# A four-layer graph network: layer 2's attention weights formed transposed, and the norms' deviations by logarithm and exponential

## The chip, the cores and the metric

The kernel runs on one core of a Trainium2 chip. The metric is the time of one execution on the device in microseconds (us), the median of several runs. One core has five engines that run beside each other, each with its own queue that is worked through in order: TensorE (PE, matrix products; its weight loads, PEld, overlap the products), VectorE (DVE), ScalarE (ACT), GpSimd (POOL) and SyncE (SP, which only issues transfers here). TensorE writes into eight banks of PSUM; the other data lie in SBUF.

## The reference

A batch of 32 graphs has 512 nodes with 128 features each, and all graphs share one 512x512 adjacency matrix. Four layers follow one another, each of the form `x = x + layer(relu(layernorm(x)))`. What the change touches is layer 2 and the layer norms:

```python
def _layernorm(x, axis=-1, eps=1e-5):
    m = jnp.mean(x, axis=axis, keepdims=True)
    v = jnp.var(x, axis=axis, keepdims=True)
    return (x - m) / jnp.sqrt(v + eps)

def _L2_gnn_ref(h, adj, W, a, bias):
    Wh = jnp.einsum('bnf,fo->bno', h, W)
    f1 = Wh @ a1;  f2 = Wh @ a2
    e = leaky_relu(f1[:, :, None] + f2[:, None, :], negative_slope=0.2)
    e = jnp.where(adj[None] > 0, e, -9e15)
    attention = softmax(e, axis=2)
    return elu(jnp.einsum('bij,bjo->bio', attention, Wh) + bias)
```

Layer 0 pairs nodes in another way and takes the softmax over the other axis. Layer 1 is the same kind of attention as layer 2, with the weights multiplied by the adjacency matrix, then a norm, a product with the adjacency matrix, a two-layer perceptron with a norm of its own, and a residual. Layer 3 applies one 512x512 matrix, the same for all graphs, to a projection.

## The kernel before

One graph is one item of work: its 512 nodes are four blocks of 128 (C = 4, H = 2), so that a tile is 128 partitions x 4 x 128 values, and such a tile fills one PSUM bank. Each item goes through `layer0`, `layer1`, `layer2`, `layer3`; all of x stays in SBUF (`xs`, one slot for each of the 32 items).

**The order of the work** isn't the order of the loops. Each step of a layer is handed to a planner (`Plan.op`) with its engine, a length in us, what it reads and what it writes. `Plan.run` then places all steps, those that can begin first, among equals the one with the earliest due time (`turn`), and the engines' queues are written in that order. The layers of different items are chains with begin times (`GAPS`); layer 1 follows layer 0 six items later, layer 2 twelve and layer 3 sixteen items later (`LAGS`). At most 20 chains are open at a time (`WINDOW`). `port=` marks steps of DVE and POOL that the planner does not let overlap. Where the planner sees PE idle for over 0.6 us, it puts throw-away products there (`idle_products`, L334).

**The norm** in front of each layer (`preln`): DVE takes mean and variance with four bn_stats and four bn_aggr (L511, L513); POOL adds the epsilon (L523) and raises to the power -0.5 (L525, `inv_dev`); the normalised tile `xn` comes from POOL (four instructions, L560), or from ACT for the first eight items of layer 0 (L545); four PE transposes (`turn_op`, L421) and an ACT Relu out of PSUM (L570) give `hT`. The perceptron's norm in layer 1 also uses `inv_dev`, and layer 1's own norm raises to -0.5 by POOL at L892.

**Attention** of layers 1 and 2 (`attend`): `project_scored` (L595) gives `h` with two more columns, the scores f1 and f2. Four PE transposes of the column f2, each broadcast over 128 columns, lay f2 out along the free axis in each partition (`repeated`, tile `prow`). Then, for each block of rows ib:

- DVE adds mask and f2 and takes the row's maximum in one instruction (L622, tile `y`),
- ACT forms the leaky ReLU (L647, f1 as bias), then the exponential with the row's maximum as bias and the row's sum accumulated (L655),
- PE turns the 128x512 block by four transposes into a bank (L421, tile `pt`), since a product needs the weights with columns j on the partitions,
- the bank is copied to `pT`: in layer 1 by DVE, times the adjacency matrix (L664); in layer 2 by ACT (L412, blocks 0 and 1) or DVE (L414, blocks 2 and 3),
- PE adds four products into `po` (L675).

`layer2` then multiplies `po` by the reciprocal of the sums (L952, L955), adds the bias on POOL (L956) and forms the elu on ACT, DVE and POOL (L960 to L962). The helper lines L421, L412, L414 and L675 are shared by layers.

An fp32 product counts as two records of MATMUL in the trace, a transpose as one: L675 has 2048 records for 2 layers x 32 items x 16 products.

Of the kernel before, what the change touches and what calls it, by code (L numbers as in the profile page):

```python
# [37 lines left out]
P = 128  # L38
# [8 lines left out]
AHEAD = 6  # L47

# [209 lines left out]
def kernel(  # L258
# [36 lines left out]
    assert F == P and C == 4 and NE % P == 0 and B >= AHEAD  # L295
# [3 lines left out]
    sm = ctx.enter_context(tc.tile_pool(name="sm", bufs=8))  # L299

# [7 lines left out]
    def small(name, shape=(P, C)):  # L308
        return sm.tile(list(shape), F32, name=name, tag=name)

# [12 lines left out]
    scored = room("scored", 6, (P, C, P2))  # L323
# [31 lines left out]
    nc.vector.memset(minus1, -1.0)  # L355
    one_b = const("one_b", (P, 1), BF16)
# [3 lines left out]
    xs = const("xs", (P, B, C, P))  # L360
# [20 lines left out]
    none = const("none", (P, C))  # L381
    maxbT = const("maxbT", (P, C))
# [14 lines left out]
    v_x = [Value() for _ in range(B)]  # L397
# [4 lines left out]
    v_offT, v_adiag, v_adiag_rep = Value(), Value(), Value()  # L402
# [4 lines left out]
    def load_x(b):  # L407
        load(lambda: xs[:, b], x[b].rearrange("(c p) f -> p c f", p=P), [v_x[b]], 1.0)
# [94 lines left out]
    def variances(src, reads):  # L503

        mv = Value()

        def emit():
            st = small("st", (P, C, 6))
            mv.own = small("mv", (P, C, 2))
            for c in range(C):  # L510
                nc.vector.bn_stats(st[:, c, :], src(c))  # L511
            for c in range(C):
                nc.vector.bn_aggr(mv.own[:, c, :], st[:, c, :])  # L513

        dve(1.1, emit, reads, [mv])
        return mv

    def inv_dev(mv):
        rstd = Value()

        def emit():
            ve = small("ve")
            nc.gpsimd.tensor_scalar(ve, mv.own[:, :, 1], LN_EPS, 1.0, ALU.add, ALU.mult)  # L523
            rstd.own = small("rstd")
# [5 lines left out]
    def preln(b, engine):  # L530

        src = xs[:, b]
        mv = variances(lambda c: src[:, c, :], [v_x[b]])
        rstd = inv_dev(mv)
        shift = Value()
        xn = value(by_act if engine is ACT else by_pool, "xn")
        if engine is ACT:

            def emit_shift():
                shift.own = small("shift")  # L540
                nc.vector.scalar_tensor_tensor(shift.own, mv.own[:, :, 0], -1.0, rstd.own, ALU.mult, ALU.mult)
# [10 lines left out]
        else:  # L552

            def emit_shift():
                shift.own = small("shift")
# [30 lines left out]
    def project_scored(hT, w_ext, reads):  # L586

        h = parts(scored, "h", 2)
        for k in range(2):
            pt = value(banks, "proj")  # L590

            def emit(k=k, pt=pt):
# [6 lines left out]
                ACT, 0.26, lambda k=k: h[k].t[:, 2 * k : 2 * k + 2, :],  # L599
# [10 lines left out]
    def attend(h, src, v_src, v_h, weights, v_weights):  # L610


        prow = repeated(lambda k: h[0].t[:, k, P + 1 : P2], h)
        y = [value(scores, "y") for _ in range(C)]
        rmax = Value()
        top = [Value() for _ in range(C)]
        for ib in range(C):

            def emit(ib=ib):
                if ib == 0:  # L620
                    rmax.own = small("rmax")
                nc.vector.tensor_tensor_reduce(  # L622
                    wide(y[ib].t), wide(prow.t), bias[:, ib, :], 1.0, LOWEST, ALU.add, ALU.max,
# [3 lines left out]
            op(DVE, 0.61, emit, [prow, v_bias], [y[ib], top[ib]])  # L627
# [12 lines left out]
        dve(0.08, emit_nmax, [ntop], [nmax], port=1)  # L640
        ssum = [Value() for _ in range(C)]
        po = parts(banks, "po", C)
        for ib in range(C):
# [18 lines left out]
            if weights is not None:  # L662
                pT = value(turned, "pT")
                op(DVE, 0.6, lambda ib=ib, pt=pt, pT=pT: nc.vector.tensor_mul(pT.t, pt.t, weights[:, :, blk(ib)]),  # L664
                   [pt, *v_weights], [pT])
            elif ib < H:
                pT = value(by_act, "pT")
                copy_op(ACT, 0.49, lambda pT=pT: pT.t, lambda pt=pt: pt.t, [pt], [pT])
            else:
                pT = value(turned, "pT")  # L670
                copy_op(DVE, 0.6, lambda pT=pT: pT.t, lambda pt=pt: pt.t, [pt], [pT])
# [15 lines left out]
    def layer0(b):  # L687
# [165 lines left out]
        dve(0.33, lambda: nc.vector.tensor_add(xs[:, b, 0:H, :], xs[:, b, 0:H, :], first[0].t[:, 0:H, :]),  # L853
            first, [v_x[b]])
        dve(0.33, lambda: nc.vector.tensor_add(xs[:, b, H:, :], xs[:, b, H:, :], terms()[:, :, 0, :]),
            second, [v_x[b]])
        op(POOL, 0.7, lambda: nc.gpsimd.tensor_add(xs[:, b, H:, :], xs[:, b, H:, :], rest.t[:, 0:H, :]),
# [3 lines left out]
    def layer1(b):  # L861
# [26 lines left out]
        rr = Value()  # L888

        def emit_rr():  # L890
            rr.own = small("rstd")
            nc.gpsimd.tensor_tensor(rr.own, ve.own, mhalf, ALU.pow)  # L892

        op(POOL, 1.0, emit_rr, [ve], [rr])
# [43 lines left out]
        op(DVE, 0.6, lambda: nc.vector.scalar_tensor_tensor(xs[:, b], res.t, 0.0, xs[:, b], ALU.max, ALU.add),  # L938
# [3 lines left out]
    def layer2(b):  # L942
        hT, _ = preln(b, POOL)
        h = project_scored(hT, w2_ext, [v_w2])
        po, ssum = attend(h, lambda: h[0].t[:, :, P], h, h, None, None)
        v1 = value(by_dve, "v1")

        rs = Value()

        def emit_rs():  # L950
            rs.own = small("rs")
            nc.vector.reciprocal(rs.own, ssum[0].own)  # L952

        dve(0.1, emit_rs, ssum, [rs])
        dve(0.6, lambda: nc.vector.tensor_mul(v1.t, po[0].t, per_chunk(rs.own)), [*po, rs], [v1])  # L955
# [6 lines left out]
        op(POOL, 1.25, lambda: nc.gpsimd.tensor_add(xs[:, b], xs[:, b], em.t), [em], [v_x[b]], port=1)  # L962


    def layer3(b):
# [6 lines left out]
        op(POOL, 1.25, lambda: nc.gpsimd.tensor_add(xb.t, xs[:, b], row_of(B_L3)), [v_x[b], v_rows], [xb], port=1)  # L972
# [22 lines left out]
    def prepare():  # L995
# [24 lines left out]
        for ib in range(C):  # L1020
            dve(0.31, lambda ib=ib: nc.vector.tensor_scalar(
                bias[:, ib, :], bias[:, ib, :], 0.0, NEG, ALU.is_le, ALU.mult), [], [v_adj[ib], v_bias], port=1)
        score_weights(lambda: wt_p.t[:, 0, :], wt_p, a1[:, 0:2], v_a1, w1_ext[:, P:P2], v_w1)
# [338 lines left out]
```

## Time and profile before

| | |
|---|---|
| time, median of 3 runs | 1062.31 us (1062.3 to 1063.7) |
| span of the profiled execution | 1062.1 us |
| PE busy | 1041.7 us, 98% |
| DVE busy | 868.5 us, 82% |
| ACT busy | 780.5 us, 73% |
| POOL busy | 776.2 us, 73% |
| granted TensorE clock, mean | 0.996 |
| first output of layer 2 (`v`, L955) | 214 us after the start |
| first output of layer 3 (`yo`, L991) | 311 us |
| last inputs of layer 0 used (`hs`, L805) | 778 us |
| last output of layer 2 / layer 3 | 1040 / 1058 us |

The profile is of one execution; its own time is taken as its span, which is 0.2 us under the median of the runs. A "group" is all instructions of one source line with the same operands: busy time of the group, mean duration of one, and the engine's idle time just before them with what ended it. Where instructions of an engine overlap, the busy time is less than the count times the mean. The "chain" is the work that ended last, followed back from the end.

### The profile page before, as it was taken

The numbers are of one execution on the slowest core, as the hardware profiler recorded it, in microseconds if no ns is written. First come the engines' busy times: TensorE is split into PE (matmuls) and PEld (weight loads), VectorE is DVE, ScalarE is ACT, GpSimd is POOL, SyncE is SP. The second block draws the span as 40 slices with busy tenths as digits, with TensorE's granted clock in tenths as the row PEclk, the third lists the DMA queues.
The fourth block names the chain that finished last, engine by engine and source line by source line (L and its number), as shares of the span: only waits on it lengthen the run. The fifth ranks groups of instructions, "written<-read, shape, count | busy, mean of one in ns | idle before, by whom it ended". The sixth has DMA issues, their size and how long they took to land.

```text
span 1062.1 us, 25166 instructions
## 1 busy us (share of the span) xinstructions
PE 1041.7 (98%) x8475; PEld 966.0 (91%) x8475; DVE 868.5 (82%) x3694; ACT 780.5 (73%) x2024; POOL 776.2 (73%) x1140
## 2 busy tenths in 40 slices
PE   7899999999999999999999999999999999999998
PEld 7789789989999999999999999999899999999997
DVE  7799999989988878888888888888888877766752
ACT  6768897789877777777877777787777777767751
POOL 4489577778787777787778778777877666576772
PEclk9899999999999999999999999999999999999999
DMA  6400000000010000000000000000000000000001
GB/s 181 96 12 2 1 2 21 2 12 11 2 31 2 21 21 21 22 21 12 2 12 11 12 12 12 11 2 11 12 11 11 11 11 11 11 22 11 22 24 37
DMA packets 56912, 20.49 MB, mean 19 GB/s; under 512 B 21584, under 2 KB 56272, under 8 KB 56784
## 3 DMA queue, kind: packets, MB, share of 16 engines
q1 hardware_dynamic: 56784, 18.90, 7.2%
q8 instruction: 67, 1.10, 0.5%
q14 instruction: 61, 0.50, 0.2%
HBM read 10.43 MB, written 8.39 MB: 18 GB/s over the span
## 4 chain that ended last, share of the span: by engine, by line
PE 88%; DVE 4%; POOL 3%; DMA 1%; SPq 1%; issue 1%; ACT 1%; POOLq 0%; DVEq 0%; ACTq 0%
PE po L675 20%; PE pt L421 16%; PE po L984 10%; PE pg L911 10%; PE proj L595 7%; PE po L837 5%; PE prow L421 3%; PE p L581 3%; PE pz L581 3%; PE px L581 3%; PE po L980 3%; PE po L842 2%; PE po L834 1%; PE po L847 1%; POOL xn L560 1%
## 5 line engine op out<-in xcount | busy, mean ns | idle before, releaser
L675 PE MATMUL po<-h,pT 128*128 128x128 f32 x2048 | 242.8, 275 | 0.8 <-DVE pT L664 0.8
L675 PEld LDWEIGHTS po<-h,pT 128*128 128x128 f32 x2048 | 236.4, 192 | 5.8 <-issue 4.1
L560 POOL TENSOR_SCALAR xn<-xs,shift,rstd 128x128 f32<-128x128 f32 x480 | 213.1, 459 | 2.8 <-DVE top L633 0.9
L655 ACT ACTIVATE y<-y,nmax 128x512 f32<-128x512 f32 x256 | 181.7, 714 | 5.3 <-DVE nmax L637 4.6
L525 POOL TENSOR_TENSOR rstd<-ve,mhalf 128x4 f32<-128x4 f32 x160 | 170.9, 1068 | 13.3
L622 DVE CUSTOM_DVE_ANT_0 y<-prow,bias 128x512 f32<-128x512 f32 x256 | 162.8, 683 | 1.6 <-PE prow L421 1.6
L984 PE MATMUL po<-h,offT 128*128 128x128 f32 x1024 | 135.4, 275 | 0.0
L911 PE MATMUL pg<-adjTe,hg 128*128 128x512 f32 x256 | 131.0, 593 | 0.0
L421 PE MATMUL pt<-ident,y 128*128 128x128 f32 x1024 | 130.2, 274 | 0.7 <-ACT hl L819 0.7
L421 PEld LDWEIGHTS pt<-ident,y 128*128 128x128 f32 x1024 | 115.1, 141 | 13.8 <-issue 8.5
L984 PEld LDWEIGHTS po<-h,offT 128*128 128x128 f32 x1024 | 124.6, 192 | 0.0
L511 DVE BATCH_NORM_STATS2 st<-xs 128x6 f32<-128x128 f32 x512 | 109.8, 277 | 7.2 <-POOL xs L962 4.5
L595 PEld LDWEIGHTS proj<-w_ext,hT 128*128 128x128 f32 x768 | 96.8, 192 | 19.0 <-issue 9.6
L595 PE MATMUL proj<-w_ext,hT 128*128 128x130 f32 x768 | 102.9, 277 | 1.4 <-ACT hT L570 1.3
L647 ACT ACTIVATE y<-y,src 128x512 f32<-128x512 f32 x128 | 84.6, 714 | 20.8 <-DVE rmax L622 19.6
L962 POOL TENSOR_TENSOR xs<-xs,em 128x512 f32<-128x512 f32 x32 | 42.0, 1312 | 76.8 <-DVE em L961 63.8
L956 POOL TENSOR_TENSOR v<-v,rows 128x512 f32<-128x512 f32 x32 | 40.9, 1279 | 72.4 <-DVE v L955 72.4
L570 ACT ACTIVATE hT<-pt 128x512 f32<-128x512 f32 x128 | 73.5, 589 | 25.3 <-PE pt L421 14.0
L647 ACT ACTIVATE y<-y,h 128x512 f32<-128x512 f32 x128 | 84.7, 714 | 7.9 <-DVE rmax L622 7.7
L664 DVE TENSOR_TENSOR pT<-pt,adjT 128x512 f32<-128x512 f32 x128 | 82.6, 681 | 5.7 <-PE pt L421 5.6
L421 PE MATMUL pt<-ident,xn 128*128 128x128 f32 x512 | 77.8, 274 | 1.5 <-POOL xn L560 1.3
L412 ACT COPY h<-proj 128x260 f32<-128x260 f32 x192 | 66.1, 371 | 13.4 <-PE proj L595 12.4
(204 smaller groups left out, 2302.3 us busy)
## 6 DMA issues: line engine op xcount, KB each, us to landing
xs<-in_x_dram SPq DMA_DIRECT2D x32, 256.0 KB, 4.0
out_dram<-yo SPq DMA_DIRECT2D x32, 256.0 KB, 2.3
u<-h SPq DMA_DIRECT2D x128, 0.5 KB, 1.8
bias<-in_adj_dram SPq DMA_DIRECT2D x4, 256.0 KB, 4.4
wts<-in_L_gnn_W_dram SPq DMA_DIRECT2D x3, 64.0 KB, 4.2
rows<-in_L_gnn_bias_dram SPq DMA_DIRECT2D x2, 64.0 KB, 3.7
wt_o<-L_gnn_others_weight_dram SPq DMA_DIRECT2D x1, 64.0 KB, 2.5
wts<-n_L_gnn_self_weight_dram SPq DMA_DIRECT2D x1, 64.0 KB, 4.5
```

The costliest lines, as they stand in the source:

```text
L421: nc.tensor.transpose(dst(k), src(k), ident)
L511: nc.vector.bn_stats(st[:, c, :], src(c))
L525: nc.gpsimd.tensor_tensor(rstd.own, ve, mhalf, ALU.pow)
L560: nc.gpsimd.tensor_scalar(xn.t[:, c, :], src[:, c, :], shift.own[:, c : c + 1], rstd.own[:, c : c + 1], ALU.add, ALU.mult,)
L581: nc.tensor.matmul(pt.t[:, c, :], lhsT=column(hT, c), rhs=w, start=True, stop=True)
L595: nc.tensor.matmul(p[:, c, :], lhsT=column(hT, 2 * k + c), rhs=w_ext, start=True, stop=True)
L622: nc.vector.tensor_tensor_reduce(wide(y[ib].t), wide(prow.t), bias[:, ib, :], 1.0, LOWEST, ALU.add, ALU.max, rmax.own[:, ib : ib + 1],)
L647: nc.scalar.activation(yw, yw, AF.Prelu, alpha=0.2, bias=src()[:, ib : ib + 1])
L655: nc.scalar.activation(yw, yw, AF.Exp, bias=nmax.own[:, ib : ib + 1], accum_out=ssum[0].own[:, ib : ib + 1])
L675: nc.tensor.matmul(po[ib].t[:, ib, :], lhsT=pT.t[:, jb, :], rhs=h[0].t[:, jb, 0:P], start=(jb == 0), stop=(jb == C - 1),)
L911: nc.tensor.matmul(wide(pg.t), lhsT=hg.t[:, nb, :], rhs=adjTe[:, nb, :], start=(nb == 0), stop=(nb == C - 1))
L984: nc.tensor.matmul(po[ib].t[:, ib, :], lhsT=offT[:, jb, blk(ib)], rhs=h1.t[:, jb, :], start=False, stop=(jb == C - 1),)
```

## The change

**Layer 2.** The weights are formed as [column j, row i] from the start, so that no transpose of them is needed. `attend` is used by layer 1 alone now; its part that finds the row maxima is the new `masked_max`, and layer 2 uses it with a result tile that nobody reads (`unused`). Two more broadcast transposes lay out f1 (`src_row`) and the negative maxima (`max_row`) along the free axis. For each block of columns jb: ACT forms the leaky ReLU out of `src_row` with f2 as bias, POOL adds the mask (`edgeT`, new, formed once from `adjT` with eight DVE instructions), DVE adds `max_row` out of PSUM, ACT takes the exponential without accumulating. `h` has a further column of ones in front (one POOL memset per item), so that the products (now 129 wide) give the row sums in their first column; the four blocks of `po` lie in two banks instead of one, and reciprocal and multiplication are done by halves.

**Norms.** `inv_dev` now runs on ACT, as exp(-0.5 ln(v + eps)), two ACT instructions of 128x4 (`inv_root`); it stays on POOL for the first eight items of layer 0. Layer 1's own norm goes the same way. One activation table set that has both functions is loaded at the start.

**Room.** `xs` has 26 slots in place of 32 (`HELD` = 26; `xs[:, b]` becomes `xs[:, b % HELD]` throughout, and item b + 26 is loaded where item b was); the small tiles of the norms rotate over 24 buffers in place of 8.

```diff
-    xs = const("xs", (P, B, C, P))
+    xs = const("xs", (P, HELD, C, P))
+    nc.scalar.preload_act_table_set("natural_log_exp_and_others")
...
+    def inv_root(var, reads, bias=None):
+        log, rstd = Value(), Value()
+        def emit_log():
+            log.own = lasting("log")
...
+                nc.scalar.activation(log.own, var(), AF.Ln, bias=bias)
+        def emit_root():
+            rstd.own = lasting("rstd")
+            nc.scalar.activation(rstd.own, log.own, AF.Exp, scale=-0.5)
+        op(ACT, 0.2, emit_log, reads, [log])
+        op(ACT, 0.2, emit_root, [log], [rstd])
+        return rstd
-    def inv_dev(mv):
+    def inv_dev(mv, engine=ACT):
+        if engine is ACT:
+            return inv_root(lambda: mv.own[:, :, 1], [mv], eps_ln)
...
-    rstd = inv_dev(mv)
+    rstd = inv_dev(mv, POOL if engine is ACT else ACT)
...
 def layer2(b):
     hT, _ = preln(b, POOL)
-    h = project_scored(hT, w2_ext, [v_w2])
-    po, ssum = attend(h, lambda: h[0].t[:, :, P], h, h, None, None)
+    h = project_scored(hT, w2_ext, [v_w2], 1)
+    ones = Value(h[0].slot)
+    op(POOL, 0.12, lambda: nc.gpsimd.memset(h[0].t[:, :, 0:1], 1.0), h, [ones])
+    prow = repeated(lambda k: h[0].t[:, k, P + 2 : P + 3], h)
+    nmax = masked_max(prow, lambda: h[0].t[:, :, P + 1], h, lambda ib: unused, lambda ib: [])
+    src_row = repeated(lambda k: h[0].t[:, k, P + 1 : P2], h)
+    max_row = repeated(lambda k: nmax.own[:, k : k + 1], [nmax])
+    pT = [value(spare, "cols") for _ in range(C)]
+    for jb in range(C):
+        def emit_leaky(jb=jb):
+            nc.scalar.activation(
+                wide(pT[jb].t), wide(src_row.t), AF.Prelu, alpha=0.2, bias=h[0].t[:, jb, P + 2 : P + 3])
+        op(ACT, 0.61, emit_leaky, [src_row, *h], pT if jb == 0 else [pT[jb]])
+        op(POOL, 1.25, lambda jb=jb: nc.gpsimd.tensor_add(
+            wide(pT[jb].t), wide(pT[jb].t), edgeT[:, jb, :]), [v_edgeT], [pT[jb]], port=1)
+        dve(0.6, lambda jb=jb: nc.vector.tensor_add(wide(pT[jb].t), wide(pT[jb].t), wide(max_row.t)),
+            [max_row], [pT[jb]])
+        op(ACT, 0.61, lambda jb=jb: nc.scalar.activation(wide(pT[jb].t), wide(pT[jb].t), AF.Exp), [], [pT[jb]])
...
+                nc.tensor.matmul(
+                    half(ib // H)[:, ib % H, 0 : P + 1], lhsT=pT[jb].t[:, ib, :], rhs=h[0].t[:, jb, 0 : P + 1],
+                    start=(jb == 0), stop=(jb == C - 1))
-    dve(0.1, emit_rs, ssum, [rs])
-    dve(0.6, lambda: nc.vector.tensor_mul(v1.t, po[0].t, per_chunk(rs.own)), [*po, rs], [v1])
+    for n in range(H):
...
+        dve(0.12, emit_rs, po[n * H : n * H + H], [rs])
+        dve(0.34, emit_v, [*po[n * H : n * H + H], rs], [v1])
...
...
+    for jb in range(C):
+        dve(0.31, ... edgeT[:, jb, :], adjT[:, jb, :], 0.0, NEG, ALU.is_le, ALU.mult ..., port=1)
+        dve(0.31, ... edgeT[:, jb, :], edgeT[:, jb, :], 0.2, None, ALU.mult ..., port=1)
```

## The prediction

> **What bounds the kernel.** I read the shares of the engines first, then the busy time by stretches, then the chain that ended last.
>
> ```profile
> PE 1041.7 (98%) x8475; PEld 966.0 (91%) x8475; DVE 868.5 (82%) x3694; ACT 780.5 (73%) x2024; POOL 776.2 (73%) x1140
> ...
> PE 88%; DVE 4%; POOL 3%; DMA 1%; SPq 1%; issue 1%; ACT 1%; POOLq 0%; DVEq 0%; ACTq 0%
> ```
>
> PE holds 88% of the chain. A busy PE need not be a PE at its peak, so the stretches must show whether it ever stands still (columns: stretch, its length, then busy time and count of PE, PEld, DVE, ACT, POOL, then clock, DMA):
>
> ```profile
> 100.00:150.00 50.00, 47.96 (x358) 42.22 (x357) 49.12 (x219) 38.54 (x107) 33.42 (x42) 1.00 0.02 2
> ...
> 200.00:250.00 50.00, 50.00 (x400) 45.50 (x400) 45.19 (x201) 41.51 (x114) 37.56 (x57) 1.00 0.03 7
> 250.00:300.00 50.00, 50.00 (x407) 46.08 (x406) 47.69 (x207) 42.69 (x113) 42.28 (x61) 1.00 0.04 7
> ...
> 500.00:800.00 300.00, 300.00 (x2477) 279.93 (x2477) 251.47 (x1049) 222.99 (x577) 233.23 (x343) 1.00 0.04 10
> ...
> 950.00:1030.00 80.00, 78.71 (x674) 75.52 (x673) 53.74 (x178) 50.92 (x114) 60.03 (x91) 1.00 0.07 21
> ```
>
> From 150 to 950 us PE never waits, at full clock. Before 125 us it does, and there the planner's throw-away products (L334, 150 of them) fill holes too; DVE is full there (49.12 of 50). So any PE work taken out after 150 us is time taken out, until another engine fills up. The chain gives PE's prices and the period:
>
> ```profile
> 601.27 3.57 PE po L675 x32
> 632.40 3.57 PE po L675 x32
> ...
> 949.64 2.62 PE pt L421 x24
> ...
> 1026.50 0.90 PE proj L595 x8
> 1027.40 0.89 PE p L581 x8
> ```
>
> One round of four layers takes 632.40 - 601.27 = **31.13 us**. A transpose costs 2.62 / 24 = 109 ns, a record of a product 3.57 / 32 = 112 ns.
>
> **PE.** Per item of layer 2, 16 transposes go (tile pt of y: 1024 for two layers, below), 8 come (src_row, max_row): -8 x 0.109 = -0.872 us. The 32 records of po become 129 wide instead of 128. No row has that width; records 130 wide take 0.90 / 8 us and 128 wide ones 0.89 / 8, so the bound is 0 to 32 x 1 ns, 0.03 us; I take 0. Over 32 items: **-27.9 us** (at least -26.9). The period would be 30.26 us, if no other engine needs more.
>
> The other engines' prices, from the groups by line (busy us, mean ns of one):
>
> ```profile
> L525 POOL TENSOR_TENSOR rstd<-ve,mhalf 128x4 f32<-128x4 f32 x160 | 170.9, 1068 | 13.3
> ...
> L421 PE MATMUL pt<-ident,y 128*128 128x128 f32 x1024 | 130.2, 274 | 0.7 <-ACT hl L819 0.7
> ...
> L664 DVE TENSOR_TENSOR pT<-pt,adjT 128x512 f32<-128x512 f32 x128 | 82.6, 681 | 5.7 <-PE pt L421 5.6
> ...
> L414 DVE COPY pT<-pt 128x512 f32<-128x512 f32 x64 | 42.9, 685 | 18.8 <-PE pt L421 18.7
> L962 POOL TENSOR_TENSOR xs<-xs,em 128x512 f32<-128x512 f32 x32 | 42.0, 1312 | 76.8 <-DVE em L961 63.8 <-DVE nmax L637 13.0
> ...
> L523 POOL TENSOR_SCALAR ve<-mv 128x4 f32<-128x4 f32 x160 | 38.3, 239 | 37.0 <-DVE mv L513 9.6 <-DVE cnt2T L477 6.7 <-DVE top L633 3.7
> ```
>
> **DVE**, per item. Two copies go (L414): -2 x 0.685 = -1.37. Four additions of a PSUM operand come, like L664: +4 x 0.681 = +2.72. The multiplication by halves: two of 0.416 (L855, 256 wide) for one of 0.687 (L955): +0.15. One more reciprocal: +0.17 (L952). Sum **+1.67**. The maxima keep their four instructions (L622, 683 ns); their result is bf16 now, for which no row of this instruction exists; I take no change, with bounds of 0.42 us each (the 256-wide form, L727) and 0.74 (the slowest 512-wide DVE row, L1232), that is -1.1 to +0.2. Today a round holds 251.47 / 300 x 31.13 = 26.1 us of DVE; after, 27.8 of 30.26, **92%**. PE ran without a gap beside a DVE at 95% (250 to 300 us), so steady rounds should still end on PE. The eight instructions for edgeT (8 x 0.43, L1021) fall where DVE is full, before 125 us, or later where they are hidden: 0 to 3.4 us.
>
> **ACT**, per item: -2 x 0.587 (copies, L412), -4 x 0.191 (accumulator reads, group L655); for six norms +12 x 0.2 (L765 0.195, L556 0.205 for a 128x4 with a pointer). Sum +0.5, on 222.99 / 300 x 31.13 = 23.1: 78% of the new round. A logarithm has no row; between the cheapest 128x4 row, 0.195, and the POOL step it replaces, 1.07, I take the former, as both are ACTIVATEs; the other end would add 5.2 us a round and bring ACT to 95%. The logarithm waits for DVE's variances at the head of ACT's queue, where L556 waits for them today (25.7 us in 29 waits); what stands behind are the exponentials and Relus that PE needs, and the 22% of slack are its cover.
>
> The page "ScalarE: Activation LUTs" (section Table sets: the hidden batching unit) says that functions of different sets cost a reload at every switch, and that one set has both exp and ln. The trace has one reload, 1283 ns. By the rule the preloaded set must also hold the leaky ReLU; were it not so, see the last rival.
>
> **POOL**: 152 pairs of L523 and L525 go, -152 x 1.307 = -198.7, and 32 powers of L892, -32 x 1.051 = -33.6. 128 mask additions come, like L962 and L956 (1.312, 1.279): +166. 32 memsets: 0.19 (POOL copy of one column, L1237) to 0.31 (256 wide, L1096), +6. Sum **-60**. A round (five inv_dev, one L892) goes from 24.2 by -7.6 and +5.4 to 22.0 us, 73%.
>
> The page "GPSIMD Engine Reference" (section 4.1, Engine selection) speaks against this: element-wise additions belong on VectorE, GpSimd being about twice slower with two inputs. The rows agree on the price (1.31 against 0.68), but on DVE the four additions would make 27.8 + 2.7 = 30.5 of 30.26, more than the round has; by time to spare the trace puts them on POOL.
>
> POOL and DVE get into each other's way where a DVE instruction has two SBUF operands:
>
> ```profile
> 602.45 0.73 POOL L857 TENSOR_TENSOR xs<-xs,rest 128x256 f32<-128x256 f32 x1 [1.14 <-DVE nmax L750]
> ...
> 602.48 0.72 DVE L754 TENSOR_TENSOR ltn<-nmax,nltm 128x4 f32<-128x4 f32 x1
> ```
>
> This 128x4 instruction, 0.16 us when free, ended with POOL's. The new DVE additions read PSUM and one SBUF tile, like L664, which kept its 0.681 us with POOL busy. POOL's instructions of this kind grow from 16.6 (24.2 - 7.6) to 22.0 us a round, so small DVE steps will meet them more often. L754 loses 0.26 us on average, L637 0.08; if twenty such steps a round each lose 0.0 to 0.1 more, that is 0 to 2 us of DVE. I take 0.5, inside its slack of 2.4.
>
> **Where the gain isn't full.** First, 200 to 300 us: layers 0, 1 and 2 run, layer 3 not yet; DVE has 92.9 of 100 us. Four items of layer 2 end there (L955 at 214, 242, 268, 293): DVE 92.9 + 4 x 1.67 = 99.6 us against PE's 100 - 3.5 = 96.5. At the 98% that DVE reaches at best (49.12 of 50) that takes 101.6, so 5.1 us are lost; layer 3 moved forward can fill some. I take **+4** (1 to 6). Second, the end: from 950 to 1030 us five items of layer 2 pass; POOL there goes from 60.0 to 60.0 + 5 x 5.4 - 11 norms x 1.307 = 72.6, of 80 - 4.4 us: 96%, and its fullest stretch so far is 92% (46.19 of 50, from 50 to 100 us). And the last item's products wait for all four blocks (3.57 us) where now only the last of 0.89 waits, and its masks take 4 x 1.3 us on POOL. I take **+3** (1 to 6). Before 125 us POOL and DVE hold the chain by turns: POOL loses about five powers between 50 and 100 us (-6.5 us of 46), DVE gains up to 3.4; I take 0 (-3 to +3.4).
>
> The slots of xs that are used again were freed four rounds before, so no load is late (layer 3 lags 16 items, loads run 6 ahead: 22 of 26), and SP gets no new transfer. The 24 buffers can only take waits away. In PSUM four banks per item (pt) go and three come (two rows, one half); no row shows PE waiting for a bank.
>
> **Sum**: 1062.1 - 27.9 + 4 + 3 + 0.5 for DVE's collisions = 1041.7 for the span; the median of the runs stands 0.2 above: **1042 us**.
>
> **Rivals.**
> (a) Collisions and waits make DVE the bound in long stretches, with part of the gain kept. Four additions per item wait in DVE's queue for POOL's mask; each wait w holds the maxima and bn_stats behind it. With w = 0.35 a round is (27.8 + 1.4) / 0.95 = 30.7, +0.47 over 26 rounds (150 to 950 us): 1042 + 12 = **1054**. For: DVE's slack is only 8%. Against: the planner knows both lengths (1.25 and 0.6) and placed the like of them today without waits (L664 loses 5.7 us in 128).
> (b) The same, beyond the break-even: (27.8 + 4w) / 0.95 = 31.13 gives w = 0.44, a third of one mask addition. With half of one, w = 0.64, a round is 32.0, +0.83 over 26 rounds, and with the 7 us of ramp and end: 1062 + 22 + 7 = **1091**. For: a DVE wait of this kind has no row. Against: POOL has 27% free.
> (c) The start gets shorter since POOL's powers go from its chain, and the ramp costs nothing: 1042 - 3 - 4 - 3 = **1032**.
> (d) The table set doesn't serve all functions: 368 reloads and more of 1.283 us put 472 us on ACT's 781 us: over **1250**.
>
> **How the numbers follow.** Forecast (1034 to 1049) 0.70; (a) 0.13; (c) 0.06; (b) 0.08; (d) 0.03. A measurement tells 0.2%, 2.1 us, from no change. Faster by more: forecast, (c) and most of (a), 0.87; within 0.2%: the edge between (a) and (b), 0.02; slower 0.11. The range takes in the forecast, (c) and most of (a): 1031 to 1056.
>
> **What would show it.** Right: transposes of L421 down by 256, rounds of 30.3 us with PE at 100%, DVE 92%, POOL 73%, one table reload. (a), (b): PE below 97% in steady rounds and DVE idle before the new addition with POOL as its releaser. The prediction is wrong if DVE's additions are dearer than L664's, or if the planner's order, changed everywhere, opens gaps on PE after 300 us.

## The result and the profile after

The changed kernel takes **1090.47 us** (median of 4 runs, 1085.44 to 1098.34) against 1062.3 for the kernel before: a ratio of 1.0271, 95% interval 1.0224 to 1.0317. It is 2.7% slower, where 2% faster was predicted. The profiled execution is the slowest of the four, 1098.34 us (span 1096.6), so what is read from its trace holds some 8 us that the median lacks.

The shares of the engines and the chain of the changed kernel:

```profile
PE 1031.5 (94%) x8233; PEld 949.0 (87%) x8233; DVE 962.0 (88%) x3831; ACT 784.7 (72%) x2200; POOL 718.3 (66%) x964
...
PE 64%; DVE 26%; ACT 5%; POOL 2%; issue 1%; DMA 1%; SPq 0%; DVEq 0%; POOLq 0%; ACTq 0%
```

PE's share of the chain fell from 88 to 64%, DVE's rose from 4 to 26%: steps of DVE now stand in PE's way. The stretches (columns as in the prediction) tell where:

```profile
50.00:100.00 50.00, 35.27 (x268) 32.79 (x267) 39.73 (x192) 33.01 (x118) 36.49 (x58) 0.83 0.04 7
...
200.00:250.00 50.00, 45.35 (x345) 39.45 (x343) 49.79 (x197) 37.59 (x116) 31.09 (x41) 1.00 0.04 7
250.00:300.00 50.00, 42.62 (x309) 38.32 (x310) 47.48 (x170) 36.93 (x100) 29.38 (x41) 0.90 0.03 6
500.00:800.00 300.00, 298.71 (x2438) 276.91 (x2437) 269.22 (x1131) 227.77 (x652) 215.22 (x294) 1.00 0.05 11
950.00:1030.00 80.00, 74.57 (x594) 69.64 (x593) 65.94 (x191) 46.75 (x109) 61.64 (x78) 0.96 0.05 14
```

PE stands still 15 us between 50 and 100, 12 between 200 and 300, 9 between 300 and 500, and 5 of the 80 from 950 on. From 500 to 900 it is full (1.3 us idle), and there the change does what it should; two products of layer 1, one round apart, in the chain:

```profile
618.21 3.57 PE po L703 x32
...
648.51 3.57 PE po L703 x32
```

A round takes 648.51 - 618.21 = **30.30 us**; 30.26 was predicted, 31.13 it was. So the loss is made before 500 us and after 900. The times of layer 3's outputs (start of `yo`, us) divide it. The forecast's column is worked out from the prediction's own terms: 0.872 us less for each layer-2 item that is through, +4 for the ramp, +3 for the end.

| | first output | 16th | last | span |
|---|---|---|---|---|
| before | 311 | 781 | 1058 | 1062.1 |
| forecast | 311 | 768 | 1037 | 1041.7 |
| after | 349 | 811 | 1093 | 1096.6 |

Of the 56 us that the last output is later than forecast, 38 were lost before the first output, 5 in the next fifteen rounds, 13 after the 16th output.

What DVE met is seen in single instructions. The timeline of the changed kernel near 310 us (columns: start, length, engine, line, operation, tile):

```profile
310.51 3.70 POOL L983 TENSOR_TENSOR cols<-cols,edgeT 128x512 f32<-128x512 f32 x3
...
310.71 4.66 DVE L664 SCALAR_TENSOR_TENSOR nmax<-top 128x4 f32<-128x4 f32 x1
...
314.17 1.17 POOL L899 TENSOR_TENSOR h<-h,row_p 128x512 f32<-128x512 f32 x1
...
315.51 0.70 PE L431 MATMUL prow<-ident,nmax 128*128 128x128 f32 x3 [3.38 <-DVE nmax L664]
```

A DVE step on 128x4 values, usually 0.16 us, takes **4.66 us**: it ends when POOL's three mask additions and the addition behind them are through. PE, which turns its result, waits 3.38 us. I call the time that DVE's instructions take over their usual length (the 20th percentile of the same line and form, counted where it is over 60 ns) **drawn-out time**. It is 27.2 us before and 71.1 after; in 22 steps it is over 1 us each, 44.6 us together (before: 3 steps). The expectations below speak of 60 us, from a first count that had missed some steps. The means of the groups show whose:

```profile
L664 DVE SCALAR_TENSOR_TENSOR nmax<-top 128x4 f32<-128x4 f32 x64 | 25.9, 404 | 0.2
...
L660 DVE SCALAR_TENSOR_TENSOR top<-rmax,h 128x4 f32<-128x4 f32 x32 | 18.7, 585 | 0.1
L774 DVE SCALAR_TENSOR_TENSOR nltm<-lt,maxbT 128x4 f32<-128x4 f32 x32 | 14.3, 447 | 0.3
```

Before, these three had means of 239, 156 and 200 ns. The step that the prediction shows, `ltn` (L782 now), fell from 420 to 221: which steps are met has changed with the order.

A gap of PE costs more than its own length here. The four longest of these steps (7.22, 5.59, 4.68 and 4.66 us) each end in a gap of PE, of 5.2, 5.4, 3.5 and 3.4 us. At each of these gaps the granted clock is 0.50 for 3.4 to 6.8 us, and products follow each other every 213 ns instead of 111. Eight records of a product take 2.08 us behind the gap that ends at 277.88, where 32 took 3.57 above:

```profile
277.88 2.08 PE po L703 x8
```

After 200 us PE has the half clock in five stretches, 23.9 us in all, and is busy for 18.7 of them. My estimate from these numbers is that half of that, 9 us, is the price of the clock in this execution. The four executions go the same way: 1085.44 us at a mean clock of 0.989, 1087.15 at 0.987, 1093.78 at 0.984, 1098.34 at 0.981.

### The profile page after: what moved, and what is told of

Same layout as the page of the kernel before. It is cut to its first block, busy times and chain, and to the rows that moved or that the text cites. A ratio compares the mean times of both kernels' runs of the same rounds, so it can differ in the third digit from the quotient of the medians.

```text
span 1096.6 us, 24657 instructions
## 1 busy us (share of the span) xinstructions
PE 1031.5 (94%) x8233; PEld 949.0 (87%) x8233; DVE 962.0 (88%) x3831; ACT 784.7 (72%) x2200; POOL 718.3 (66%) x964
## 4 chain that ended last, share of the span: by engine, by line
PE 64%; DVE 26%; ACT 5%; POOL 2%; issue 1%; DMA 1%; SPq 0%; DVEq 0%; POOLq 0%; ACTq 0%
PE po L1048 10%; PE pt L431 8%; PE pg L933 7%; PE po L997 7%; PE po L703 6%; PE proj L626 5%; PE prow L431 5%; DVE st L521 4%; PE po L865 4%; DVE unused L649 3%; PE po L1044 2%; DVE pT L698 2%; PE p L612 2%; PE po L870 2%; PE px L612 2%; ACT y L805 2%
## 5 line engine op out<-in xcount | busy, mean ns | idle before, releaser
L983 POOL TENSOR_TENSOR cols<-cols,edgeT 128x512 f32<-128x512 f32 x128 | 164.7, 1310 | 46.2 <-ACT cols L978 44.6
L703 PEld LDWEIGHTS po<-h,pT 128*128 128x128 f32 x1024 | 119.5, 193 | 13.3 <-issue 7.2
L703 PE MATMUL po<-h,pT 128*128 128x128 f32 x1024 | 121.6, 276 | 5.2 <-DVE pT L698 5.2
L997 PEld LDWEIGHTS po<-h,cols 128*128 128x128 f32 x1024 | 118.5, 192 | 4.8 <-issue 3.8
L997 PE MATMUL po<-h,cols 128*128 128x129 f32 x1024 | 121.2, 275 | 0.0
L987 ACT ACTIVATE cols<-cols 128x512 f32<-128x512 f32 x128 | 77.2, 629 | 39.1 <-DVE cols L985 38.5
L690 ACT ACTIVATE y<-y,nmax 128x512 f32<-128x512 f32 x128 | 90.8, 712 | 7.0 <-DVE rs L1010 5.6
L985 DVE TENSOR_TENSOR cols<-cols,prow 128x512 f32<-128x512 f32 x128 | 81.5, 677 | 14.0 <-POOL cols L983 6.7
L649 DVE CUSTOM_DVE_ANT_0 unused<-prow,bias 128x512 bf16<-128x512 f32 x128 | 87.9, 687 | 5.1 <-PE prow L431 1.8
L649 DVE CUSTOM_DVE_ANT_0 y<-prow,bias 128x512 f32<-128x512 f32 x128 | 81.5, 682 | 1.0 <-PE prow L431 0.8
```

Source lines behind the costliest of these rows:

```text
L649: nc.vector.tensor_tensor_reduce(out(ib), wide(prow.t), bias[:, ib, :], 1.0, LOWEST, ALU.add, ALU.max, rmax.own[:, ib : ib + 1],)
L690: nc.scalar.activation(yw, yw, AF.Exp, bias=nmax.own[:, ib : ib + 1], accum_out=ssum[0].own[:, ib : ib + 1])
L703: nc.tensor.matmul(po[ib].t[:, ib, :], lhsT=pT.t[:, jb, :], rhs=h[0].t[:, jb, 0:P], start=(jb == 0), stop=(jb == C - 1),)
L983: op(POOL, 1.25, lambda jb=jb: nc.gpsimd.tensor_add(wide(pT[jb].t), wide(pT[jb].t), edgeT[:, jb, :]), [v_edgeT], [pT[jb]], port=1)
L997: nc.tensor.matmul(half(ib // H)[:, ib % H, 0 : P + 1], lhsT=pT[jb].t[:, ib, :], rhs=h[0].t[:, jb, 0 : P + 1], start=(jb == 0), stop=(jb = ...
```

## The experiments

The theories: **C**, collisions: DVE's small steps stand still beside POOL's mask additions. **D**: DVE is simply full with layer 2's new additions. **R**: it is full in the ramp only. **N**: the norms on ACT, whose logarithms stand at the head of ACT's queue, hold up what PE needs. **L**: the planner's order fell out unluckily. Ratios are to the kernel before on the same chip, with 95% intervals.

### Which half of the change

`l2_only` has the new layer 2 and leaves the norms on POOL; `norms_only` has layer 2 as before, and the norms, the 26 slots and the 24 buffers of the change.

```diff
 l2_only
-    def inv_dev(mv, engine=ACT):
+    def inv_dev(mv, engine=POOL):
-    rstd = inv_dev(mv, POOL if engine is ACT else ACT)
+    rstd = inv_dev(mv)
```

> The new layer 2 with all norms back on GpSimd. Theory R (ramp): until layer 3 joins, layers 0 to 2 now need more DVE than PE, so most of the loss stays: 1068 to 1085 us, PE full again from 50 to 100 us, gaps of PE between 200 and 400 us, first output of layer 3 still 20 us or more later than before. Theory N (norms): the logarithms that wait at the head of ScalarE's queue for DVE's variances hold up the Relus and copies that PE needs: 1035 to 1050 us.

> Layer 2 as before, norms by logarithm and exponential on ScalarE (with 26 slots of x and the 24 small buffers of the changed kernel). R: only the gap of 15 us between 75 and 100 us can be of the norms: 1062 to 1076 us, PE full from 200 to 900 us. N: 1080 to 1100 us, PE with gaps all along.

Measured: `l2_only` 1079.41 us, 1.0162 (1.0147 to 1.0177); `norms_only` 1071.34, 1.0083 (1.0068 to 1.0098). Each half loses by itself. `norms_only` has a full PE from 200 to 900 us and loses before 100, where PE stands for 11.9 us of 50 instead of 1.6; its drawn-out time is 30.3 us. `l2_only` loses all along, with 64.7 us drawn out and POOL busy for 286 of the 300 us from 500 to 800, so that a full POOL is a second possible cause there. Both times lie in the ranges of R and outside those of N, though R's signs for `l2_only` did not come (PE full from 50 to 100 us, where it was busy for 41.6 of 50; the first output 20 us late, where it was 15). So N is a matter of the start, and the larger loss belongs to layer 2.

### DVE's load, and the order

`no_max_add` leaves out the subtraction of the maxima, with its transposes; `thin_add` shrinks DVE's four additions to four columns in the unchanged order; `lag14` starts layer 3 two items earlier.

```diff
 no_max_add
-    max_row = repeated(lambda k: nmax.own[:, k : k + 1], [nmax])
-            dve(0.6, lambda jb=jb: nc.vector.tensor_add(wide(pT[jb].t), wide(pT[jb].t), wide(max_row.t)), ...)
 thin_add
+            ... nc.vector.tensor_add(pT[jb].t[:, 0, 0:4], pT[jb].t[:, 0, 0:4], max_row.t[:, 0, 0:4])
 lag14
-GAPS, LAGS = (5.3, 12.0, 6.7, 5.4), (0, 6, 12, 16)
+GAPS, LAGS = (5.3, 12.0, 6.7, 5.4), (0, 6, 12, 14)
```

> The changed kernel without the subtraction of the row's maximum in layer 2 (the four DVE additions and the four transposes of max_row are left out; the maxima are still formed). DVE loses 4 x 0.65 = 2.6 us per item and PE 0.44. R: layers 0 to 2 fit PE again and the ramp's 20 us come back, with the 14 us of the transposes: 1035 to 1055 us. N: the ScalarE queue is the same, only the transposes go: 1072 to 1082 us.

> The changed kernel in its own order; the 128 DVE additions of the row's maximum are left at four columns (0.1 instead of 0.64 us, 70 us of DVE in all), so the maximum is not subtracted. D: the slip after 150 us is gone, 1045 to 1060 us. C: the collisions remain (DVE's drawn-out time still 50 us or more), but DVE has slack to take them up between 150 and 500 us: 1060 to 1078 us.

> The changed kernel with layer 3 planned 14 instead of 16 items behind layer 0, no other edit. R: layer 3, which is rich in PE and poor in DVE work, fills PE's gaps some 60 us earlier: first output of layer 3 before 320 us, time 1065 to 1080 us. N: no change, 1083 to 1100 us. If only the drawn order of the planner was unlucky (theory L), any new order may give 1040 to 1095.

Measured: `no_max_add` 1090.4, 1.0269 (1.0254 to 1.0285); `thin_add` 1084.02, 1.0199 (1.0174 to 1.0225); `lag14` 1076.93, 1.0142 (1.0125 to 1.0158). Without DVE's new additions most of the loss stays, and the drawn-out time too (92.7 and 77.9 us), against D and R. These two runs don't settle it. In `no_max_add`, which has another order, the loss lies elsewhere: 4 us of PE's gaps between 200 and 300 us, but 21 between 500 and 800. `thin_add`, in the unchanged order, missed C's range as well (1060 to 1078): DVE's new slack did not take the collisions up. And `lag14` came out as R had it, in time and with the first output at 283 us; the order is worth 13.5 us, with 66.1 us still drawn out. What decides against D and R as the main cause is the next run, `thin_mask`: DVE keeps all its additions (890 us busy besides what is drawn out, as in the changed kernel).

### Taking the mask additions off the way to SBUF

Three kernels with the planned lengths, and so the order of the first two, unchanged. `thin_mask` adds the mask on four columns; `pow_mask` puts a 128x4 power, about as long as an addition, in its place. Both leave the mask out. `berth` does all the work and makes the planner keep 0.2 us between steps of POOL and DVE that it will not let overlap.

```diff
 thin_mask
-            ... nc.gpsimd.tensor_add(wide(pT[jb].t), wide(pT[jb].t), edgeT[:, jb, :]), [v_edgeT], [pT[jb]], port=1)
+            ... nc.gpsimd.tensor_add(pT[jb].t[:, 0, 0:4], pT[jb].t[:, 0, 0:4], edgeT[:, jb, 0:4]), ...)
 pow_mask
+            ... nc.gpsimd.tensor_tensor(pT[jb].t[:, 0, 0:4], pT[jb].t[:, 0, 0:4], zeros, ALU.pow), ...)
 berth
-HOLD = 0.05
+HOLD = -0.2
```

> As pow_mask, but the mask additions are left at four columns (0.1 to 0.2 us of GpSimd instead of 1.3). C: like pow_mask, 1055 to 1072 us. D: 1082 to 1098 us. If it is far below pow_mask, it is the latency or the load of GpSimd and not the collisions.

> The changed kernel in its own order on every queue; only the 128 mask additions on GpSimd (128x512, 1.3 us, two SBUF inputs) are replaced by as many powers of four columns (128x4, about 1.05 us), so the mask is not applied. GpSimd is nearly as long busy, but hardly moves data. Theory C (collisions): DVE's small steps with two SBUF operands get stuck behind GpSimd's additions, up to 1.25 us each, and the queues that both PE and DVE fill to the brim pass the delay on. DVE's drawn-out instructions fall from 60 us to 35 us or less in all, time 1058 to 1074 us. Theory D (DVE is simply full with layer 2's additions): no change, 1082 to 1098 us.

> The changed kernel with one constant of the planner changed: HOLD -0.2 instead of 0.05, so that DVE's and GpSimd's steps that must not overlap are planned 0.2 us apart. All work is done. C: few collisions (DVE's drawn-out time under 30 us): 1035 to 1055 us, faster than before. D: 1075 us or more. L (only the drawn order was unlucky): anywhere from 1040 to 1090 us, with collisions as in the changed kernel.

Measured: `thin_mask` 1058.9, 0.9969 (0.9957 to 0.9981); `pow_mask` 1059.43, 0.9972 (0.9962 to 0.9982); `berth` 1086.32, 1.0222 (1.0201 to 1.0243). The stretches of `thin_mask`:

```profile
200.00:250.00 50.00, 49.61 (x385) 44.12 (x384) 48.93 (x216) 41.08 (x123) 26.37 (x45) 1.00 0.04 7
250.00:300.00 50.00, 47.47 (x371) 42.09 (x370) 45.91 (x202) 43.76 (x127) 28.51 (x51) 1.00 0.03 7
```

PE's gaps of 12 us between 200 and 300 us shrink to 3, drawn-out time is 28.8 us. 31.6 us of the changed kernel go with the data that POOL's mask additions move. It is not their length: the power is nearly as long, draws DVE out no more (29.5 us), and gives the same time. `berth` missed what C had expected of it, under 30 us drawn out and 1035 to 1055. In its order a planned distance does not help (drawn-out time 97.7 us): the planner already keeps these steps apart on paper, but nothing holds POOL to that on the chip, where it runs ahead to its next addition.

### Holding POOL to the plan

`guard` does all the work in the order of the changed kernel: a step of POOL marked `port` waits, by a semaphore, for the last such step of DVE that the plan has before it. `guard_before` puts the same into the kernel before. `split4` cuts each mask addition into four.

```diff
 guard, guard_before
+            if op.port and op.engine is POOL and self.yielded is not None:
+                tc.add_manual_dep(mine, self.yielded.name, ... DependencyClass.Sync ...)
+            if op.port and op.engine is DVE:
+                self.yielded = [i for i in traced[first_new:] if i.engine == mybir.EngineType.DVE][-1]
 split4
+                for k in range(4):
+                    own = bass.ts(k, 128)
+                    nc.gpsimd.tensor_add(wide(pT[jb].t)[:, own], wide(pT[jb].t)[:, own], edgeT[:, jb, own])
```

> The changed kernel in the same order on every queue; each step of POOL that the planner gave the shared way to SBUF (the mask additions, L956, L962 and their like) waits by a semaphore for the last such step of DVE that the planner put before it, so that it can no longer run ahead of it. All work is done. Collisions (C): the time that DVE's instructions take over their usual one falls from 60 us to 35 or less, and the time from 1090 to 1060-1075. D (DVE is simply full) and L (an unlucky order): 1085 to 1095, since neither the work nor the order is touched. If the semaphores themselves cost POOL more than the collisions cost DVE: above 1090, with POOL idle before its additions and DVE as their releaser.

> Control: the same waits put into the kernel before, whose DVE has 26 us of drawn-out time, most of it not beside PE's path. All theories: within 1055 to 1064; a fall of more than 8 us would say that the waits help whatever the change does, a rise that they cost something by themselves.

> The changed kernel with each mask addition of POOL cut into four of 128 columns. All work is done, planned with 1.7 us for the four. C, if a DVE step that meets one waits for the end of that one instruction: a wait is at most about 0.45 us instead of 1.25, the drawn-out time of DVE falls to 30-45 us, and the time to 1060-1078. If DVE's step gets no turn between the pieces: as the changed kernel, 1085 to 1098. POOL has 0.4 us more per addition, 50 us more in all; if POOL then bounds the start and the end: up to 6 us of the gain is lost.

Measured: `guard` **1061.78**, 0.9993 (0.9984 to 1.0002); `guard_before` 1062.82, 1.0009 (0.9999 to 1.0018); `split4` 1114.35, 1.0490 (1.0473 to 1.0506). The stretches of `guard`:

```profile
200.00:250.00 50.00, 50.00 (x391) 44.76 (x390) 48.28 (x204) 40.31 (x119) 32.33 (x40) 1.00 0.04 7
250.00:300.00 50.00, 47.49 (x368) 41.85 (x367) 47.52 (x194) 41.73 (x118) 37.20 (x52) 1.00 0.04 6
...
950.00:1030.00 80.00, 78.50 (x660) 74.24 (x660) 63.58 (x203) 48.20 (x114) 72.39 (x96) 1.00 0.07 21
```

With nothing changed but who goes first, 29 us come back, between 200 and 500 us and at the end (outputs at 326, 785 and 1056 us); the control gains nothing. PE has no half clock between 95 and 1055 us any more, so that the gain holds the clock's share too. **C is shown** for the changed kernel, with all the work done. One expectation missed: drawn-out time only falls to 52.9 us, not to 35. But no step is drawn out by more than 1.4 us any more (six were, by 27.4 us together), and PE's wait for `nmax` between 200 and 600 us falls from 9.5 to 2.3 us.

The sum of drawn-out time does not order the runs: `breath` below has 58.8 us and takes 1079.6, `guard_edge_p20` has 60.1 and takes 1055.0; `guard_before` halves the 27.2 of the kernel before to 13.2 and gains nothing. The few long steps do better. Steps drawn out by over 1.4 us are none before, none in `thin_mask`, `pow_mask` and `guard`, six in the changed kernel and eleven (31.3 us) in `split4`. That it is these, and not the many short ones, was not tried by itself.

`split4` missed both its ranges: 99.7 us drawn out, with steps that stand through up to nine POOL instructions in a row, 5.0 us. Its planned lengths differ (1.7 us for 1.25), and so its order; why it is so slow stays open.

### Who waits for what

`probe` and `probe_order` put stretches behind the last output of the kernel before, in which POOL and DVE run beside each other; only the second holds the written order in all stretches, and I read that one. `breath` is the changed kernel with a memset behind each mask addition. Two readings compete: **O**, a DVE step goes at the end of the addition that it meets; **T**, it goes only when POOL stops.

```diff
 breath
+                nc.gpsimd.memset(junk4, 1.0)
 probe_order: the DVE steps, eight in a stretch
+    def two():   nc.vector.tensor_add(little, little, pc)
+    def three(): nc.vector.scalar_tensor_tensor(little, little, 0.5, pc, ALU.mult, ALU.max)
+    def one():   nc.vector.tensor_scalar(little, little, 0.5, None, ALU.mult)
+    def psum():  nc.vector.tensor_add(little, little, bank[:, 0, 0:C])
```

> The kernel before, and behind its last output eight stretches, each started by one ACT copy, in which POOL and DVE run beside each other: DVE always eight 128x4 steps, POOL (1) to (3) six 128x512 additions back to back, with DVE steps of two SBUF operands, of one, and of one SBUF and one PSUM operand; (4) to (8) DVE steps of two SBUF operands beside twelve POOL additions of 128 columns, additions with a memset between, with a multiplication by a number between, with a power between, and six powers alone. In the traces so far DVE steps were found standing through up to six POOL additions. No turn between back-to-back additions (T): in (1) the first DVE step, or all eight, end only after the sixth addition, some 7 us; in (4) after the twelfth; (2), (3) and (8) are free, 0.15 to 0.2 us a step. One addition each (O): in (1) each DVE step waits for at most one addition, 1.3 us, in (4) 0.45 us. What (5) to (7) show is open: if a step in between lets DVE in, its wait falls to one addition.

> The changed kernel in the same order, with a memset of 128x4 (about 0.1 us) behind each of POOL's mask additions; all work is done. T, with the memset letting DVE in: no DVE step takes over 1.4 us longer than usual (five did, 20 us in all), and the time falls by 8 to 20 us, to 1070-1083. T, with the memset letting nobody in, or O: as the changed kernel, 1085 to 1098, up to 10 us more by POOL's 128 more steps.

> The eight stretches of probe again, behind the last output of the kernel before, now with each engine's order held as written and DVE starting about 0.7 us after POOL. POOL: 128x512 additions back to back (1 to 4, 8), additions in pieces of 128 columns (5), with a memset of 128x4 behind each (6), with a 128x4 power behind each (7). DVE: eight 128x4 steps of (1) two SBUF operands, (2) two in the other form of instruction, (3) one SBUF operand, (4) one SBUF and one PSUM operand, (5 to 7) as (1), (8) two of (4) ahead of each of (1). O (a step goes at the end of the POOL addition that it meets): 1.15 to 1.2 us a step in (1), (2), (6), 0.4 in (5), about one in two at 0.16 in (7). T (it goes when POOL stops): the first step of (1), (2), (5), (6) ends with POOL's last addition, 5 to 9 us. Both at times, as the kernels' traces have it (302 steps went at the first end, 35 after two to six): mostly 1.2, single ones longer. Stretch (4) free. Stretch (3): free, if only two SBUF operands meet POOL; 1.2 us a step, if one is enough.

The timeline of `probe_order`: POOL's and DVE's lines of the stretches (1), (3), (4) and (5).

```profile
1054.01 9.82 POOL L1362 TENSOR_TENSOR bias<-bias,adjT 128x512 f32<-128x512 f32 x8 [4.68 <-DVE adjT L1394]
1054.30 9.54 DVE L1376 TENSOR_TENSOR probe_s<-probe_s,probe_c 128x4 f32<-128x4 f32 x8
...
1076.15 9.59 DVE L1382 TENSOR_SCALAR probe_s<-probe_s 128x4 f32<-128x4 f32 x8
...
1087.23 1.50 DVE L1385 TENSOR_TENSOR probe_s<-probe_s,probe_bank 128x4 f32<-128x4 f32 x8
...
1098.05 3.12 DVE L1376 TENSOR_TENSOR probe_s<-probe_s,probe_c 128x4 f32<-128x4 f32 x8
```

Eight steps need 9.54 us: 1.19 us each, one POOL addition, as O has it. One SBUF operand is enough in this form of instruction (9.59 us); with one operand in PSUM the eight are free (1.50 us); beside additions a quarter as wide they wait 0.38 us each (3.12). A memset between the additions changes nothing (1.22 us a step); beside a power five steps of 0.16 us passed. The page "SBUF — State Buffer" of the Trainium skill (section SBUF: two separate sides) says that POOL and DVE share one pair of ports as a lock, held for a whole instruction by whichever starts first; it names DVE instructions in a two-port mode or with two SBUF inputs. That agrees with the 1.19 us and with the free steps on PSUM. It does not cover two things here: the power, which reads SBUF too and holds nobody up, and the steps that stood through several instructions.

For in the kernels both outcomes occur. Counted from the instruction records of 13 profiles (DVE steps of 128x4 that last over 0.22 us and start inside a POOL step which another one of over 0.7 us follows without a gap): 302 steps went at the first end, 35 only after two to six. There are 7 such meetings before, 33 after, 7 in `guard`. What decides between the outcomes stays **open**. `breath` took 1079.63, 1.0162 (1.0145 to 1.0179), in the range that T had named, and yet two steps of 5.6 and 2.6 us remained, and in the probe the memset changed nothing; why it gains 11 us is open too. That the meetings are partly chance fits the spread of the runs, 13 us for the changed kernel and 4 for `guard`, but is not shown by it.

### What else stands between 1062 and the forecast

`guard_p16` takes the norms of the first 16 items of every layer back to POOL; `guard_edge_p16` also forms `edgeT` later, behind the 15th layer of the planner's order (layer 0 of the eleventh item), at 109 to 128 us instead of 15 to 22; `guard_edge_p20` has 20 items in place of 16; `guard_l2` is `guard` with all norms on POOL.

```diff
 guard_p16 (20 in guard_edge_p20)
-    rstd = inv_dev(mv, POOL if engine is ACT else ACT)
+    rstd = inv_dev(mv, POOL if b < 16 else ACT)
 guard_edge_p16, guard_edge_p20 (the eight DVE steps move out of prepare)
+        if n == 14:
+            late_edge()
```

> As guard, and the norms of the first 16 items of every layer take the two POOL steps of the kernel before again, those of the other 16 the logarithm and exponential on ACT. All work is done. Norms at the start (N) and collisions (C) as two separate losses: another 5 to 12 us below guard, 1048 to 1062, with PE's idle time between 50 and 100 us down from 14.7 to 8-11 us. If the start's loss does not come from the norms: as guard. If the collisions alone were the whole loss: as guard within 4 us.

> guard_p16 with the eight DVE steps that make edgeT moved from the first 25 us of the program to behind the ninth step of the loop over items; all work is done. If these 3.4 us of DVE lie on the path of the start, as the prediction bounded them (0 to 3.4 us): 1053 to 1057, with PE's idle time of the first 100 us down from 15.7 by 3 to 5 us. If they are hidden: 1058 to 1060.

> guard_edge_p16 with the norms of the first 20 items on POOL instead of 16; all work is done. The planner's own end is 3.5 us earlier, by 5 us less PE idle time in its last 50 us. If the end is limited as the planner has it: 1050 to 1053. If POOL's 19 us more in the steady rounds collide and wait: 1054 to 1060.

> guard with all the norms of the kernel before (POOL's two steps), so layer 2's new form alone without collisions by additions that run ahead; all work is done. Without guard it took 1079.4. Collisions as the main loss of l2_only too: 1050 to 1064. POOL (945 us busy) as its own bound: 1065 to 1080, with POOL above 92% and PE waiting for POOL's masks or norms.

Measured: `guard_p16` 1059.12, 0.9969 (0.9958 to 0.9981); `guard_edge_p16` **1054.83**, 0.9921 (0.9907 to 0.9936); `guard_edge_p20` 1055.02, 0.9920 (0.9907 to 0.9934); `guard_l2` 1088.0, 1.0236 (1.0220 to 1.0251). The stretch from 50 to 100 us, of `guard` and then of `guard_edge_p16`:

```profile
50.00:100.00 50.00, 34.86 (x266) 31.91 (x264) 37.21 (x185) 32.53 (x117) 36.20 (x58) 0.86 0.04 7
```

```profile
50.00:100.00 50.00, 47.69 (x393) 44.31 (x393) 45.78 (x221) 37.46 (x115) 46.79 (x80) 1.00 0.07 12
```

Of PE's 15 idle us at the start 2.3 are left. In `guard` 8.8 of them were one wait of layer 0's products for a copy on ACT (`h`, L434); by the timeline ACT had softmax steps of other items ahead of it (L694, L702). That the quicker norms let these through is my reading. `guard_p16` by itself gained 2.7 us where 5 to 12 were expected, though PE's idle time there fell from 15.1 to 7.1 us; between 500 and 800 us its PE lost 2.7 us against 0.9 in `guard`. Four more items on POOL change nothing. `guard_l2` missed: it was expected at 1050 to 1064, or with POOL above 92% at 1065 to 1080. It is 8.6 us slower than `l2_only`, so here the waits cost more than they save. Between 500 and 800 us:

```profile
500.00:800.00 300.00, 287.28 (x2329) 265.19 (x2328) 275.35 (x1093) 202.54 (x515) 276.20 (x380) 1.00 0.04 9
```

POOL is busy for 92%, and PE loses 12.7 us. That such a POOL has no room left to wait for DVE is argued, not tried by itself. But `guard` and `guard_l2` differ in the norms alone, by 26 us: with these waits the new layer 2 needs the norms off POOL in the rounds.

`guard_edge_p16` beats both kernels: all the work done, 0.8% under the kernel before. Its outputs stand at 318 (first), 781 (16th) and 1049 us (last).

## Why the prediction was wrong

**Right, by its own steps.** PE: rounds of 30.30 us at a full PE. DVE's busy time without what is drawn out went from 841.3 to 890.9 us; less 3.4 for `edgeT` that is 1.44 us an item (1.67). Its additions out of PSUM took 677 ns (681), the maxima with a bf16 result 687 (683). POOL fell by 58 us (60). ACT rose by 4 us, or 0.13 an item (0.5); a logarithm with epsilon as a pointer took 299 ns (152 of them), without it 197, the root 204. The prediction took 195, and L556's 205 for a step with a pointer; the row of L556 reads `mv` alone. One table load, so rival (d) fell. From 500 to 800 us POOL stood at 72% and DVE at 90%. The rule that only two SBUF operands meet POOL was too narrow: in `probe_order` a multiplication by a number, with one, waits 1.19 us too.

**The step that failed** is the one for the collisions: "I take 0.5, inside its slack of 2.4". It saw the mechanism and put it into the sum with 0.5 us for the whole execution; `guard` gives 29. The size of DVE's delay was within its bounds: 71.1 - 27.2 = 43.9 us of drawn-out time more over 32 items, in the slowest execution, 1.4 us a round where 0 to 2 had been allowed. Wrong was the cover, that DVE's slack of a steady round hides it. The time does not fall evenly: 30.7 of the 71.1 us fall between 200 and 450 us and 17.7 between 900 and 1050, where DVE has no slack or PE waits for the very step, and single ones took 1.2 to 7.2 us, not a mean of 0.1. The estimate went by how long POOL is busy with such instructions (16.6 to 22.0 us a round). What it did not count is that layer 2 issues four additions back to back: 33 meetings with a run of additions, where there were 7, and six steps that stood through two to six of them. Nor did it give a gap of PE a price beyond its length; about 9 us of the trace are the half clock behind such gaps. Price in all: 29 us (`guard`) to 31.6 (`thin_mask`), of the 48 us by which the forecast missed.

**The other terms.** The start was put at 0 (-3 to +3.4) because POOL and DVE held the chain there. With faster norms the largest wait there is another, PE for ACT's copy, and `edgeT` on DVE lies in the path: together 7 us by `guard_edge_p16` (norms 2.7, `edgeT` 4.3 against its bound of 3.4). The remaining 13 us to the forecast: by the outputs of `guard_edge_p16` against the forecast's row, 7 before the first output and 6 in the next fifteen rounds; what makes them was not tried. The end's +3 was right once the collisions were out (268 us from the 16th output to the last, 269 in the forecast).

**The rivals.** (b) named 1091 us; that the time came true is luck, for the cause was a different one. It had DVE's additions wait for POOL's masks, in every round, and a round of 32.0 us. The waits of the changed kernel show little of that:

```profile
DVE cols L985 <- POOL cols L983: 6.7, 9, 1.4
```

6.7 us in 9 waits, the longest 1.4, and 30.30 us a round. The same two engines, but POOL's additions in the way of other items' small steps.

## What to carry to other kernels

When work goes to POOL, count which DVE steps can stand beside it, not how long both are busy: here each small step that met an addition waited at least for its end, and with four additions back to back the meetings went from 7 to 33. The planner's rule that two steps don't overlap held on the chip only with a semaphore behind it. And slack of a steady round is no cover for the ramp and the end, so a cost that is put "inside the slack" needs a place.

## What the runs showed of the hardware

- A 128x4 DVE step that meets a 128x512 POOL addition ends some 20 ns behind that addition; steps in a row take 1.19 us each instead of 0.16. It holds for one SBUF operand in a multiplication by a number as for two, and not if one operand lies in PSUM. POOL's power (1.02 us) holds nobody up.
- In the kernels a step can miss the end of the addition and stand through several: 7.2 us through six POOL instructions at the most.
- Cutting the additions into four made the kernel slower by 24 us, although a piece holds up a step for only 0.38 us in the probe; its planned order differs too.
- In the changed kernel the granted clock was 0.50 for 3.4 to 6.8 us at each of four gaps of PE of 3.4 to 5.4 us, and products took 213 ns each instead of 111. Averaged over 50 us it is 0.83 with 35.27 us busy, 0.90 with 42.62, but 1.00 with 45.35. The same start without the gaps (47.69 busy) had 1.00.
